# A stack of three preactivated convolutions and one rational filter: two batches instead of one take a tile from products shared by pixel pairs

## The chip, the cores and the metric

The kernel runs on one core of a Trainium2 chip. The metric is the device time of one execution in microseconds. The engines have rows of their own: TensorE (PE, with its weight loads as PEld), VectorE (DVE), ScalarE (ACT), GpSimd (POOL) and SyncE (SP), which only issues DMAs. Each engine works its row in the order in which the program lists it; an instruction that waits holds up everything behind it on that engine. DMAs are issued from SP, ACT and POOL and stand in those rows too.

## The reference

Four layers follow one another, each `x = x + layer(norm(x))` on `x` of 4 batches x 32 x 32 pixels x 16 channels. `norm` is a group norm over 8 groups of 2 channels. The first three layers have this form, with `M` and `Wp` of 1024 x 1024 and a 3x3 kernel `G` of its own for each of the 1024 output pixels:

```
first   = einsum('ijpq,bpqc->bijc', M2, inputs)
K       = transpose(G, (2, 3, 4, 0, 1, 5)).reshape(kh, kw, c, h*w*f)
shifted = conv(inputs, K, 'SAME').reshape(b, h, w, h, w, f)
diff    = relu(inputs[:, :, :, None, None, :] - shifted)
second  = einsum('ijpq,bpqijc->bijc', W2, diff)
return first - second
```

So each output pixel has its own convolution over the whole image, a Relu, and a weighted sum over the 1024 pixels. That makes 1024 x 16 filter outputs over 1024 pixels for each batch and layer. The last layer is a two-dimensional filter given as a ratio of polynomials, worked out as an impulse response and applied by matmuls.

## The kernel before

**Blocks and tiles.** The 1024 x 16 filters of a layer are 128 blocks of 128. A *tile* is one block for one batch: 128 filters on the partitions, 1024 pixels as two halves of 512 columns in PSUM. `iteration` (line 653) makes one tile: TensorE computes it, then VectorE *evicts* it with one instruction (line 658), which takes the minimum with 0, multiplies by the weights `wts` and sums over the pixels into `acc`.

**Two kinds of tile.** `SHARED` (line 19) says for each batch which kind it is. A `direct` tile (line 594) runs the nine taps over all 512 columns of a half: two float32 products of four taps each, `f`, and one of the ninth tap as high and low pieces in float32r, `g` (line 609). A `shared` tile (line 614) works on pairs of neighbouring pixels: products common to both are computed once on 256 columns into a PSUM buffer `both` (line 625), ScalarE copies that to SBUF as `both_sb` (line 629), TensorE computes the pixels' own part (line 637), and VectorE adds `both_sb` to it in PSUM (line 645) before the eviction. Only batch 3 is shared. All PSUM tiles, `pt`, come from one pool of four buffers (line 51); a shared tile takes two of them.

**Order.** `passes` (line 85) lists what runs. A layer has its first 12 blocks for batches 0 and 1, then the same blocks for batches 2 and 3, then the 104 middle blocks with all four batches in turn, then the last 12 blocks for 0 and 1 and again for 2 and 3. The split gives time to make the next layer's image of two batches while the other two still run. `order` is the list of all 1536 tiles, `now["at"]` the place in it, `begin[u]` where chunk `u` of four blocks begins, and `need` where a chunk's other taps are needed.

**Work beside the tiles.** It is written as generators. After every tile `iteration` calls `step` (line 586), which moves each one on; `until(at)` waits for a place in the order. So the code says after which tile an instruction is listed, and each engine keeps that order:

- `four_taps` (485) loads `f` of a chunk and has GpSimd subtract the middle tap.
- `other_taps` (499) loads the tap table `raw`; after 4 to 7 tiles GpSimd subtracts the middle tap and adds (lines 506 to 508), one tile later ScalarE casts `hi` (512), one later GpSimd makes `lo` (514) and issues eight DMAs to DRAM (519). `piece_loads` (524) loads them back as `g` on SP, one tile of 128 x 512 for a chunk without a shared batch, six with one (12 DMAs).
- `w_loads` (576) loads the weights, 1 MB for two blocks, from six buffers.
- `make_image` (309), `store_image` (342) and `load_image` (380) make the next layer's image of a pair of batches: norm, copies and differences on ScalarE, GpSimd and VectorE, three DMAs to DRAM, and 28 DMAs back, taken in turn by SP and POOL for batches 0 and 1 and by SP, POOL and ACT for 2 and 3.
- `first_term` (419) makes the product with `M`; `impulse_response` (724), beside layer 0's middle, makes the filter of the last layer, much of it on GpSimd.

**The opening.** The host gives the taps of batches 0 and 1 unnormalised. `first_images` (192) normalises and masks them in SBUF for the first pass; its `rest` makes the image of batches 2 and 3 during that pass. The loads are listed from line 864 on.

Of the kernel before, what the change touches and what calls it, by code (L numbers as in the profile page):

```python
# [18 lines left out]
SHARED = (False, False, False, True)  # L19
# [17 lines left out]
def conv_stack_kernel(ctx, tc, x, M, W, first_w, first_f, first_g, F, E, h0, coef, cst, dft, idp, idq, out):  # L37
# [10 lines left out]
    ge = ctx.enter_context(tc.tile_pool(name="ge", bufs=1))  # L48
    junkp = ctx.enter_context(tc.tile_pool(name="junk", bufs=1))
# [22 lines left out]
    ye = [const.tile([P, row[a]], F32, name=f"ye{a}") for a in range(2)]  # L72
    for t in (*yp, *ye):
        nc.gpsimd.memset(t, 0.0)
# [10 lines left out]
    passes = [  # L85
        (blks, batches)
        for layer in range(3)
        for blks, batches in (
            (range(layer * NBLK, layer * NBLK + END), (0, 1)),
            (range(layer * NBLK, layer * NBLK + END), (2, 3)),  # L90
            (range(layer * NBLK + END, (layer + 1) * NBLK - END), (0, 1, 2, 3)),
            (range((layer + 1) * NBLK - END, (layer + 1) * NBLK), (0, 1)),
            (range((layer + 1) * NBLK - END, (layer + 1) * NBLK), (2, 3)),
        )
    ]
# [9 lines left out]
    now = {"at": 0}  # L105
# [86 lines left out]
    def first_images(nine, g9):  # L192
# [21 lines left out]
        def last_tap(b):  # L214
            v, v8 = nine[:, b], ims_of(b)[1].rearrange("p l m -> p (l m)")
            m = neg[:, B + b : B + b + 1]
            nc.vector.tensor_scalar(v8, v, m, rstd[:, B + b : B + b + 1], ALU.add, ALU.mult)
            nc.vector.tensor_scalar(v, v, m, rlo[:, b : b + 1], ALU.add, ALU.mult)
            nc.vector.scalar_tensor_tensor(v8, v8.bitcast(F32), sign, v, ALU.mult, ALU.add)
            nc.gpsimd.memset(  # L220
                ims_of(b)[1].rearrange("p l (cc x) -> p (l cc) x", x=S)[:, :, S - 1 :].bitcast(F32), 0.0
            )

        def first_taps(u):
            part = g9[:, bass.ts(u, GC * P)]
            nc.scalar.copy(gn0[u], part)
            for r in (32, 96):
                lo = gn0[u][r : r + 32]
                nc.vector.tensor_tensor(lo, part[r : r + 32], lo.bitcast(F32), ALU.subtract)
            gt[u] = [gn0[u]]  # L230
# [30 lines left out]
        minus_mid(fours[0][:, 1].rearrange("r (n f) -> r n f", f=C), mid, nc.vector)  # L261
# [4 lines left out]
        for _ in range(2):  # L266
            next(norm)
        dft(0, 1)
# [8 lines left out]
        normalise(0, 0, nc.vector)  # L277
        clear(0, 0)
        normalise(0, 1, nc.scalar)
        clear(0, 1)  # L280
# [3 lines left out]
        last_tap(0)  # L284
        for k in range(2):
            normalise(1, k, nc.vector)
            clear(1, k)
        last_tap(1)

        def rest():  # L290

            yield
            yield
            first_taps(1)
            yield
            pair = lambda a: (xs[:, 2 * a : 2 * a + 2], *(t[:, 2 * a : 2 * a + 2] for t in (neg, rstd)))
            yield from store_image(1, *pair(1))
            yield
            load_image(0, 1)
            copy_out(1)  # L300
            yield
            center(0, *pair(0))
            yield
            copy_out(0)
            nc.vector.tensor_copy(avg_r, avg)
# [3 lines left out]
    def make_image(layer, a, xt):  # L309

        xt = xt[:, 2 * a : 2 * a + 2]
        neg, rstd = yield from group_norm(xt)
        yield from store_image(a, xt, neg, rstd)
        yield
        load_image(layer + 1, a)
        copy_out(a)
# [25 lines left out]
    def store_image(a, xt, neg, rstd):  # L342
# [27 lines left out]
        for b, v in enumerate(kinds):  # L370
            to = kinds_of(ye[a], a, b)
            nc.gpsimd.tensor_copy(to[96:, :, 1:], v[96:, :, :3])
            nc.scalar.copy(to[:32, :, :3], v[:32, :, 1:])
        rows = img[a]
# [5 lines left out]
    def load_image(layer, a):  # L380

        moves = []
        of = lambda t: t.rearrange("p l k m -> p l (k m)")
        for b in range(2):
# [26 lines left out]
        queues = (nc.sync, nc.gpsimd, nc.scalar)[: 2 + a]  # L411
        for n, (to, src) in enumerate(moves):
            queues[n % len(queues)].dma_start(out=to, in_=src)  # L413
# [71 lines left out]
    def four_taps(u):  # L485

        at = max(begin[u] - 30, begin[u - 2] if u > 2 else 0)
        if u == 1:
            at = 2
        yield from until(at)  # L490
        load_f(u)
        yield from until(min(max(at + 8, begin[u] - 16), begin[u] - 2))
        minus_mid(fours[u][:, 1].rearrange("r (n f) -> r n f", f=C), mid)
# [5 lines left out]
    def other_taps(q, at):  # L499

        layer, ch = divmod(q, NBLK // GC)
        yield from until(at[0])
        raw = ge.tile([96, 3, 2 * P], F32, tag="raw", name="raw")
        nc.sync.dma_start(out=raw.rearrange("r k n -> r (k n)"), in_=E[layer][ch])
        yield from until(at[1])
        minus_mid(raw[:, 1].rearrange("r (n f) -> r n f", f=C), mid_e)
        for k in (1, 2):
            nc.gpsimd.tensor_tensor(raw[:, 0], raw[:, 0], raw[:, k], ALU.add)  # L508
        yield from until(at[1] + 1)
        both = raw[:, 0::2]  # L510
        hi, lo = (ge.tile([96, 2, 2 * P], F32R, tag=tag, name=tag) for tag in ("hi", "lo"))
        nc.scalar.copy(hi, both)  # L512
        yield from until(at[1] + 2)
        nc.gpsimd.tensor_tensor(lo, both, hi.bitcast(F32), ALU.subtract)  # L514
        to = gd[q % len(gd)]
        for k, t in enumerate((hi, lo)):
            for u in range(2):
                for slot in range(2):
                    nc.gpsimd.dma_start(  # L519
                        out=to[slot, :, k, :, bass.ts(u, 2 * P)],  # L520
                        in_=t[48 * u : 48 * u + 48, slot].bitcast(F32),
                    )

    def piece_loads(u):

        q, first, sharing = uses[u]
        yield from until(max(begin[u - 1], first - 12))
        tiles = [gn.tile([P, GC * P], F32R, tag=f"g{n}", name=f"g{n}") for n in range(6 if sharing else 1)]
        gt[u] = tiles
        to = gd[q % len(gd)]  # L530
        rows = (1, 0, 2), (1, 2, 0), (1, 1, 1), (0, 0, 0), (0, 1, 1), (0, 2, 2)
        for t, (slot, *dys) in zip(tiles, rows):
# [6 lines left out]

    tasks = []  # L540
    at = 0, 1
    for q in sorted(need, key=need.get):
        tasks.append((at[0], other_taps(q, at)))
        following = [k for k in sorted(need, key=need.get) if need[k] > need[q]][:1]
        for k in following:
            first = max(need[k] - 26, at[1] + 3)
            at = first, max(first + 4, min(first + 7, need[k] - 9))
# [28 lines left out]
    def w_loads():  # L576
        while len(wts) < len(w_first):
            k = len(wts)
            yield from until(w_first[k] - (24 if k > 5 else 10))
            while not w_free():  # L580
                yield
            list(load_w())
# [69 lines left out]

    def iteration(layer, acc):
        blk, b, u = order[now["at"]]
        assert blk // NBLK == layer
        pt = (shared if SHARED[b] else direct)(layer, u, blk, b)
        junk = junkp.tile([P, S * S], F32, tag="junk", name="junk")
# [9 lines left out]
        now["at"] += 1  # L667
        step()

    def conv_layer(layer, xt, finish, side=(), also=iter(())):  # L670
# [11 lines left out]
        for job, (blks, batches) in enumerate(passes[5 * layer : 5 * layer + 5]):  # L682
            for blk in blks:
                for _ in batches:
                    iteration(layer, acc)
                if job == 2:
# [5 lines left out]
            if job > 2:  # L692
                a = batches[0] // 2
# [170 lines left out]
    with tc.tile_pool(name="st", bufs=1) as st:  # L864
        table = st.tile([P, B], F32, name="table")
# [3 lines left out]
        image_tiles(0, 0)  # L869
        image_tiles(0, 1)  # L870
        nine = st.tile([P, 2, 4 * PX], F32, name="nine")
        g9 = st.tile([P, 2 * GC * P], F32, name="g9")
        first_part = 4 * P + 2 * NCH
        coefs = st.tile([P, coef.shape[1]], F32, name="coefs")
        for part in (slice(0, first_part), slice(first_part, coef.shape[1])):
            nc.sync.dma_start(out=coefs[:, part], in_=coef[:, part])
# [4 lines left out]
        nc.scalar.dma_start(out=g9[:, : GC * P], in_=first_g[:, : GC * P])  # L881

        def load_first(b):
            size = 8 * PX
            for to, at in ((ims[0, b][0].rearrange("p l k m -> p (l k m)"), 0), (nine[:, b], 8 * PX)):
                nc.sync.dma_start(out=to, in_=first_f[:, b, at : at + size])
                size = 4 * PX

        load_f(0)
        load_first(0)  # L890
        list(load_w(2))
        load_first(1)
        nc.sync.dma_start(out=g9[:, GC * P :], in_=first_g[:, GC * P :])
# [15 lines left out]
    FIRST = 24  # L909
# [18 lines left out]
    def of_pair(a, k, q):  # L928
# [3 lines left out]
            (("pair", a), 2 * i + half, y(31 - TQ * k - q - i + 16 * half - FIRST), k, q + i)  # L932
# [28 lines left out]
    def norm3(_, a, xt):  # L961
# [15 lines left out]
        if a == 0:  # L977
            yq = work.tile([P, 16 * (31 + S - FIRST)], F32, name="yq")
# [20 lines left out]
        for y in (  # L999
            late["yp"][:, a, :, 31 - FIRST :],  # L1000
# [21 lines left out]
    tp = ctx.enter_context(tc.tile_pool(name="tp", bufs=TB))  # L1022

# [5 lines left out]
    def toeplitz():  # L1029
        for k in held[:TB]:  # L1030
# [29 lines left out]
    for n, slot in enumerate(then):  # L1060
        if n in (2, 4, 5):
            k = {2: 4, 4: 3, 5: last}[n]
            list(load_toeplitz(k, toeplitz_tile(k, tp)))
# [173 lines left out]
```

## Time and profile before

| | us |
|---|---|
| three runs, median (lowest to highest) | 3047.37 (3042.73 to 3047.81) |
| the profiled execution, its own time | 3047.96 |
| its span, first to last instruction | 3046.2 |
| L609 matmuls of direct tiles, float32: busy, mean of one | 2239.4, 0.592 |
| L637 matmuls of shared tiles, float32 and float32r: busy | 509.8 and 503.4 |
| L658 evictions: busy, mean of one, count | 1880.8, 1.224, 1536 |
| L645 additions of `both_sb`: busy, mean, count | 473.1, 1.232, 384 |
| L629 copies to `both_sb`: busy, mean, count | 224.9, 0.586, 384 |
| L512 casts on ScalarE: busy, mean, count | 59.3, 0.618, 96 |
| GpSimd: busy in all | 1070.6 |

A line of a group in the profile has the code line, the engine, the operation, `out<-in` and the shapes. A timeline row has the start and length in us, the engine, the code line, the operation, how many instructions of that kind are merged in it, and in brackets how long the engine had stood idle before and what ended that. Busy times of TensorE overlap, as its two halves of 64 rows work at once; the distance between the first matmuls of two tiles is the time of a tile. The granted clock of TensorE is 1.00 in the middle of the layers and 0.91 in the first 100 us.

### The profile page before, as it was taken

Reading aid. Unit: us, or ns where it says so; the run is one execution under the profiler, and the core shown is the slowest. Engines: PE = TensorE matmul, PEld = TensorE weight load, DVE = VectorE, ACT = ScalarE, POOL = GpSimd, SP = SyncE. Lnnn points to the kernel's source line nnn. Section 1 sums busy time; section 2 is a strip of 40 time slices with the busy share of each in tenths; the row PEclk is TensorE's granted clock in tenths of the full one; section 3 lists DMA queues with packets and bytes.
Section 4 is the critical chain, followed back from the end, with each engine's and each line's share of the span. In section 5 each row is a group of like instructions: output and inputs, shape, how many; then the busy total and the mean of one; then the engine's idle time right before and its main releaser. Section 6 shows DMA issues by size and latency. Waiting matters only on the chain.

```text
span 3046.2 us, 53601 instructions
## 1 busy us (share of the span) xinstructions
PE 2982.4 (98%) x20884; PEld 2192.1 (72%) x20884; DVE 2412.9 (79%) x3639; ACT 307.5 (10%) x555; POOL 1070.6 (35%) x1517
## 2 busy tenths in 40 slices
PE   7999999999999899999999999989999999999998
PEld 4765666788887576678888888757567888888874
DVE  5878888888887787788888888769788888888873
ACT  1110110000001011000000100101000000000000
POOL 5435663232332433432323233343333233332300
PEclk8999999999999999999999999999999999999998
DMA  8887676656675898766666676589777776857634
GB/s 233 230 207 185 158 189 167 178 154 169 162 164 146 209 224 200 182 155 168 165 158 173 150 180 150 157 198 235 197 179 178 167 185 163 199 151 180 151 107 80
DMA packets 235589, 531.82 MB, mean 175 GB/s; under 512 B 83672, under 2 KB 93496, under 8 KB 209992
## 3 DMA queue, kind: packets, MB, share of 16 engines
q1 hardware_dynamic: 162832, 472.72, 61.3%
q0 software_dynamic: 66480, 47.05, 6.7%
q10 hardware_dynamic: 6024, 8.63, 1.4%
q8 instruction: 165, 2.70, 0.4%
q14 instruction: 88, 0.72, 0.1%
HBM read 481.67 MB, written 45.92 MB: 173 GB/s over the span
## 4 chain that ended last, share of the span: by engine, by line
PE 84%; DVE 3%; DMA 2%; issue 1%; SPq 0%; ACT 0%; POOL 0%; DVEq 0%; POOLq 0%; ACTq 0%
PE pt L609 65%; PE pt L637 14%; PE pt L625 3%; DVE junk L658 2%; PE pt L952 1%; DVE pt L645 1%; DMA f<-img 1%; DMA t<-hd 1%; PE pt L445 0%; DMA g<-gd 0%; SPq L535 0%; DMA raw<-in_E_dram 0%; SPq L413 0%; DVE st L150 0%; POOL raw L508 0%
## 5 line engine op out<-in xcount | busy, mean ns | idle before, releaser
L609 PE MATMUL pt<-f,f 64*128 64x512 f32 x9216 | 2239.4, 592 | 10.3 <-DVE junk L658 4.0
L658 DVE SCALAR_TENSOR_TENSOR junk<-pt,w 128x1024 f32<-128x1024 f32 x1536 | 1880.8, 1224 | 372.7 <-PE pt L609 256.1
L609 PEld LDWEIGHTS pt<-f,f 64*128 64x128 f32 x9216 | 1149.1, 187 | 503.6 <-issue 264.6
L609 PE MATMUL pt<-n,g 64*128 64x480 f32 x2304 | 997.0, 779 | 6.3 <-DMA g<-gd 6.2
L645 DVE TENSOR_TENSOR pt<-pt,both_sb 128x1024 f32<-128x1024 f32 x384 | 473.1, 1232 | 195.2 <-PE pt L637 164.4
L637 PE MATMUL pt<-f,f 64*128 64x256 f32 x3072 | 509.8, 378 | 3.5 <-DVE junk L658 1.2
L637 PE MATMUL pt<-n,g 64*128 64x256 f32 x3072 | 503.4, 372 | 0.0
L629 ACT COPY both_sb<-pt 128x512 f32<-128x512 f32 x384 | 224.9, 586 | 2350.5 <-PE pt L625 2265.3
L609 PEld LDWEIGHTS pt<-n,g 64*128 64x128 f32 x2304 | 314.9, 188 | 188.5 <-issue 102.9
L475 POOL TENSOR_TENSOR raw<-raw,cs 96x256 f32<-96x256 f32 x96 | 69.8, 727 | 908.6 <-DMA raw<-in_E_dram 908.3
L637 PEld LDWEIGHTS pt<-n,g 64*128 64x128 f32 x3072 | 370.2, 188 | 6.3
L514 POOL TENSOR_TENSOR lo<-raw,hi 96x512 fp32r<-96x512 f32 x96 | 121.9, 1270 | 529.3 <-ACT hi L512 529.3
L637 PEld LDWEIGHTS pt<-f,f 64*128 64x128 f32 x3072 | 293.6, 186 | 4.8 <-PE pt L625 2.6
L625 PEld LDWEIGHTS pt<-n,g 64*128 64x128 f32 x2304 | 230.8, 186 | 83.1 <-issue 35.9
L625 PE MATMUL pt<-n,g 64*128 64x256 f32 x2304 | 230.3, 279 | 20.2 <-ACT both_sb L629 20.2
L519 POOL DMA_DIRECT2D gd<-lo x384 | 226.8, 597 | 12.8 <-DMA f<-img 8.1
L519 POOL DMA_DIRECT2D gd<-hi x384 | 229.6, 603 | 3.2 <-issue 3.2
L475 POOL TENSOR_TENSOR f<-f,cs 128x512 f32<-128x512 f32 x113 | 145.6, 1289 | 192.3 <-DMA f<-in_F_dram 167.5
L508 POOL TENSOR_TENSOR raw<-raw 96x256 f32<-96x256 f32 x192 | 139.5, 727 | 15.1
L658 DVE DVE_READ_ACCUMULATOR junk<-pt,w 128x1 f32 x1536 | 127.8, 83 | 0.0
L512 ACT CAST hi<-raw 96x512 fp32r<-96x512 f32 x96 | 59.3, 618 | 189.2 <-POOL raw L508 189.0
L461 POOL DMA_DIRECT2D fd<-ft x48 | 25.2, 533 | 44.2 <-ACT ft L453 27.2
(131 smaller groups left out, 341.2 us busy)
## 6 DMA issues: line engine op xcount, KB each, us to landing
w<-in_W_dram SPq DMA_DIRECT2D x188, 1024.0 KB, 12.1
g<-gd SPq DMA_DIRECT2D x1184, 128.0 KB, 4.3
f<-in_F_dram SPq DMA_DIRECT2D x114, 512.0 KB, 3.6
raw<-in_E_dram SPq DMA_DIRECT2D x96, 288.0 KB, 9.3
gd<-hi POOLq DMA_DIRECT2D x384, 48.0 KB, 4.2
gd<-lo POOLq DMA_DIRECT2D x384, 48.0 KB, 4.5
mt<-in_M_dram SPq DMA_DIRECT2D x12, 512.0 KB, 12.7
w<-in_M_dram SPq DMA_DIRECT2D x12, 512.0 KB, 8.0
```

The lines of the kernel that those rows point to most:

```text
L475: engine.tensor_tensor(v, v, m.unsqueeze(1).to_broadcast([v.shape[0], v.shape[1], C]), ALU.subtract)
L508: nc.gpsimd.tensor_tensor(raw[:, 0], raw[:, 0], raw[:, k], ALU.add)
L512: nc.scalar.copy(hi, both)
L514: nc.gpsimd.tensor_tensor(lo, both, hi.bitcast(F32), ALU.subtract)
L519: nc.gpsimd.dma_start(out=to[slot, :, k, :, bass.ts(u, 2 * P)], in_=t[48 * u : 48 * u + 48, slot].bitcast(F32),)
L609: nc.tensor.matmul(pt[:, half, px], lhsT=w[rows, at], rhs=rhs, start=k == 0, stop=k == 2)
L625: nc.tensor.matmul(both[:, half], lhsT=w[rows, at], rhs=ni[rows, dy : dy + 4, 2], start=dy == 0, stop=dy == 2)
L629: nc.scalar.copy(sb, both)
L637: nc.tensor.matmul(pt[:, half].rearrange("p (r k m) -> p k r m", k=2, m=16)[:, k], lhsT=w[rows, at], rhs=rhs, start=k == j == 0, stop=k == ...
L645: nc.vector.tensor_tensor(v, v, sb.rearrange("p h (r m) -> p (h r) m", m=16).unsqueeze(2).to_broadcast([P, 32, 2, 16]), ALU.add,)
L658: nc.vector.scalar_tensor_tensor(junk, pt.rearrange("p h m -> p (h m)"), 0.0, wts[blk // 2][:, blk % 2, :], ALU.min, ALU.mult, accum_out=a ...
L952: nc.tensor.matmul(rows.rearrange("n (j r) -> n j r", j=C)[:, :, 8 * cc :], lhsT=y(cc).rearrange("p q b -> p (q b)"), rhs=ts[k][q][:, :, : ...
```

## The change

1. Batch 1 becomes shared too; a block then has two direct tiles (0, 2) and two shared ones (1, 3). In the last and first 12 blocks the pass of batches 0 and 1 has one of each, as that of 2 and 3 had, and needs all six `g` tiles.
2. `by_pool` picks one eviction in four: in the middle batch 2, in layer 0's first 12 blocks batch 1, in the other end passes the direct batch of every second block. `by_gpsimd` does it in three steps: ScalarE writes Relu(-pt) to SBUF as `r`, GpSimd multiplies by the weights in place, and ScalarE, listed four tiles later by `finish_sums`, copies `r` with scale -1 and sums it into `acc`.
3. In `other_taps` the cast `hi` moves from ScalarE to GpSimd and everything from the subtraction to the eight DMA issues is listed at one place. `raw` has two buffers and is asked for up to 34 tiles ahead of need, and worked on 15 ahead. `lo` takes its place.
4. `piece_loads` asks for the five tiles of shared batches as soon as their own buffers allow, and for the first one as before.
5. The first pass of layer 0 has batches 0 and 2 (`FIRST`), both direct, and the second 1 and 3, both shared. `rest` makes an image of both pairs, one after the other, and loads only batch 1 and batch 3 of them. The loads of the opening come in another order, some tiles move to other buffers, and the first `f` loses its middle tap on GpSimd instead of VectorE.
6. `load_image` issues one batch's 14 DMAs after each of two tiles, on SP and POOL alone. While an image is stored and loaded (`now["image"]`), `w_loads` issues nothing.

The core of the diff:

```diff
-SHARED = (False, False, False, True)
+SHARED = (False, True, False, True)
+FIRST = (0, 2)
...
+    er = ctx.enter_context(tc.tile_pool(name="er", bufs=2))
+    rp = ctx.enter_context(tc.tile_pool(name="rp", bufs=2))
...
-        normalise(0, 0, nc.vector)
+        normalise(FIRST[0], 0, nc.vector)
...
+            for a in range(2):
+                pair = slice(2 * a, 2 * a + 2)
+                at = xs[:, pair], neg[:, pair], rstd[:, pair]
+                later = [b for b in range(2) if 2 * a + b not in FIRST]
+                if later:
+                    yield from store_image(a, *at)
+                    yield
+                    yield from load_image(0, a, later)
...
-        queues = (nc.sync, nc.gpsimd, nc.scalar)[: 2 + a]
-        for n, (to, src) in enumerate(moves):
-            queues[n % len(queues)].dma_start(out=to, in_=src)
+            queues = nc.sync, nc.gpsimd
+            for n, (to, src) in enumerate(moves):
+                queues[n % len(queues)].dma_start(out=to, in_=src)
+            yield
+        now["image"] -= 1
...
-        raw = ge.tile([96, 3, 2 * P], F32, tag="raw", name="raw")
+        raw = er.tile([96, 3, 2 * P], F32, tag="raw", name="raw")
...
-        yield from until(at[1] + 1)
         both = raw[:, 0::2]
-        hi, lo = (ge.tile([96, 2, 2 * P], F32R, tag=tag, name=tag) for tag in ("hi", "lo"))
-        nc.scalar.copy(hi, both)
-        yield from until(at[1] + 2)
+        hi, lo = ge.tile([96, 2, 2 * P], F32R, tag="hi", name="hi"), both.bitcast(F32R)
+        nc.gpsimd.tensor_copy(hi, both)
         nc.gpsimd.tensor_tensor(lo, both, hi.bitcast(F32), ALU.subtract)
...
+        first = max(need[q] - 34, done[-2])
+        at = first, max(first + 3, need[q] - 15, done[-1])
...
-            while not w_free():
+            while not w_free() or now["image"]:
...
+    def by_pool(blk, b):
+        if END <= blk % NBLK < NBLK - END:
+            return b == 2
+        if blk < END:
+            return b == 1
+        return not SHARED[b] and blk % 2 == 0
+
+    def by_gpsimd(pt, blk, to):
+        r = rp.tile([P, S * S], F32, tag="r", name="r")
+        nc.scalar.activation(r, pt.rearrange("p h m -> p (h m)"), AF.Relu, scale=-1.0)
+        nc.gpsimd.tensor_tensor(r, r, wts[blk // 2][:, blk % 2, :], ALU.mult)
+        sums_due.append((now["at"] + 4, r, to))
+
+    def finish_sums(all=False):
+        while sums_due and (all or sums_due[0][0] <= now["at"]):
+            _, r, to = sums_due.pop(0)
+            nc.scalar.activation(r, r, AF.Copy, scale=-1.0, accum_out=to)
...
         pt = (shared if SHARED[b] else direct)(layer, u, blk, b)
+        if by_pool(blk, b):
+            by_gpsimd(pt, blk, acc[b // 2][:, b % 2, blk % NBLK : blk % NBLK + 1])
+            return
...
                     iteration(layer, acc)
+                    now["at"] += 1
+                    finish_sums()
+                    step()
```

## The prediction

> **What bounds the kernel now.** I read the page's engine shares and its chain first, then a stretch of windows, then one block in the timeline, then the costliest groups, the waits, and the stretches at a layer's end.
>
> ```profile
> PE 2982.4 (98%) x20884; PEld 2192.1 (72%) x20884; DVE 2412.9 (79%) x3639; ACT 307.5 (10%) x555; POOL 1070.6 (35%) x1517
> PE pt L609 65%; PE pt L637 14%; PE pt L625 3%; DVE junk L658 2%; PE pt L952 1%; DVE pt L645 1%; DMA f<-img 1%; DMA t<-hd 1%; PE pt L445 0%; DMA g<-gd 0%; SPq L535 0%; DMA raw<-in_E_dram 0%; SPq L413 0%; DVE st L150 0%; POOL raw L508 0%
> ...
> 2500.00:2900.00 400.00, 400.00 (x2762) 326.08 (x2758) 328.01 (x481) 37.32 (x65) 128.13 (x177) 1.00 0.68 170
> ```
>
> The chain is matmuls: 65% direct tiles (line 609), 17% shared ones (637, 625). In the window (PE, weight loads, DVE, ACT, POOL, then clock and DMA) TensorE is busy all 400 us at clock 1.00, VectorE 82%, GpSimd 32%. So in the middle of a layer TensorE sets the pace and a tile's price is the distance between tile starts:
>
> ```profile
> 1502.55 0.52 PE L625 MATMUL pt<-n,g 64*128 64x256 f32 x5
> ...
> 1504.24 0.59 PE L609 MATMUL pt<-f,f 64*128 64x512 f32 x1
> ...
> 1506.17 1.88 PE L609 MATMUL pt<-f,f 64*128 64x512 f32 x7
> ...
> 1510.04 0.52 PE L625 MATMUL pt<-n,g 64*128 64x256 f32 x5
> ```
>
> A shared tile takes 1504.24 - 1502.55 = 1.69 us, a direct one (1510.04 - 1504.24) / 3 = 1.933; three and one make a block of 7.49. Where only batches 2 and 3 run, VectorE is the pace:
>
> ```profile
> 2952.23 1.23 DVE L645 TENSOR_TENSOR pt<-pt,both_sb 128x1024 f32<-128x1024 f32 x1
> 2953.49 1.23 DVE L658 SCALAR_TENSOR_TENSOR junk<-pt,w 128x1024 f32<-128x1024 f32 x1
> ...
> 2954.83 1.23 DVE L658 SCALAR_TENSOR_TENSOR junk<-pt,w 128x1024 f32<-128x1024 f32 x1
> ...
> 2955.98 1.23 DVE L645 TENSOR_TENSOR pt<-pt,both_sb 128x1024 f32<-128x1024 f32 x1
> ```
>
> An addition holds it 1.26, an eviction 1.34 before another eviction and 1.15 before an addition: 3.75 per pair of tiles, where TensorE needs 3.62. Last, the ScalarE wait at a layer's end and the GpSimd work of one chunk:
>
> ```profile
> 1015.44 0.62 ACT L512 CAST hi<-raw 96x512 fp32r<-96x512 f32 x1 [15.27 <-POOL raw L508]
> 1015.96 0.57 ACT L629 COPY both_sb<-pt 128x512 f32<-128x512 f32 x1
> ...
> 1500.88 0.72 POOL L475 TENSOR_TENSOR raw<-raw,cs 96x256 f32<-96x256 f32 x1 [11.69 <-DMA raw<-in_E_dram]
> 1501.69 1.53 POOL L508 TENSOR_TENSOR raw<-raw 96x256 f32<-96x256 f32 x2
> 1511.90 1.27 POOL L514 TENSOR_TENSOR lo<-raw,hi 96x512 fp32r<-96x512 f32 x1 [8.68 <-ACT hi L512]
> 1513.12 2.38 POOL L519 DMA_DIRECT2D gd<-hi  x4
> 1515.49 2.36 POOL L519 DMA_DIRECT2D gd<-lo  x4
> 1517.87 1.30 POOL L475 TENSOR_TENSOR f<-f,cs 128x512 f32<-128x512 f32 x1
> ```
>
> The cast stood in ScalarE's row before a `both_sb` copy and waited for a late tap load; TensorE stood still twice for it, 20.2 us together.
>
> **What the change takes away.** Batch 1 becomes shared: in the middle stages 3 layers x 104 blocks x (1.933 - 1.69 = 0.243) = -75.9 us. Five end passes of batches 0 and 1 (three at a layer's end, two at its start), 12 blocks each: -14.6. Five passes of batches 2 and 3 fall from VectorE's 3.75 to TensorE's 3.62, since half of the direct tiles leave VectorE: 5 x 12 x 0.13 = -7.8. The cast leaves ScalarE's row: -20.2. Together -118.5.
>
> **Whether the other engines hold that pace.** VectorE per middle block: evict, add, evict, add, evict = 1.15 + 1.26 + 1.15 + 1.26 + 1.34 = 6.16 of TensorE's 7.25. ScalarE: two copies of 0.59, the new Relu (the 128x1024 PSUM copy of line 788 took 1.02), the summing copy. The last has no row: at least the 1.02, at most that plus two of VectorE's 0.08 accumulator reads and a small ACTIVATE of 0.20, so 1.02 to 1.4; I take 1.2, near the plain copy. Sum 3.4. Relu stands nowhere in this trace; a table load for it and another back (1.28 each, line 867) would make 6.0, still under 7.25. GpSimd: the product is 128x1024; 256 columns take 0.73, 512 take 1.29, so 1.29 + 2 x 0.56 = 2.41 (2.3 to 2.6, by the rows' spread). `hi` on GpSimd: its 32x480 copy took 0.58, the two-operand form 1.27; one operand, so 0.62, bounds 0.6 and 1.27. A chunk of four blocks then holds 9.7 of products, a burst of 2.3 + 0.62 + 1.2 + 4.75 plus gaps = 9.1 (two adds, cast, subtraction, eight DMA issues, now in one piece) and 1.3 for `f`: 20 of 29.0 us. On average all fit; what counts is the order in the queues.
>
> The Trainium skill (GPSIMD Engine Reference, 4.1) speaks against the product's place: elementwise work belongs on VectorE, GpSimd being about twice as slow with two inputs. The row agrees, 2.41 against 1.22; on VectorE it would close the block at 7.5, no faster than now. The skill (SBUF — State Buffer, two separate sides) also says that GpSimd and a VectorE instruction with two SBUF inputs lock each other out. The evictions read one input from PSUM, and that of 1501.08 took 1.23 beside GpSimd's 1501.69 as others do alone; with a lock 384 products would cost VectorE up to 384 x (2.41 - 1.09 idle) = 500 us, by the row nothing.
>
> **What it adds on the path.** The summing copy waits in ScalarE's row for the product; behind it stand the next Relu and the next `both_sb` copy, for which VectorE's addition waits, and TensorE for its PSUM buffer.
>
> *Chunk by chunk.* From the chunk's first tile: Relu 5.9 to 6.9, product to 9.4, burst to 18.5, second product to 20.9, its sum to 22.1; the third block's Relu, due at 20.4, ends at 23.1, its copy at 23.7, so an addition due at 22.15 comes 1.55 late. VectorE regains 1.09 per block. If PSUM's four buffers go round in fixed order, TensorE loses 1.1 us per chunk (the tile that starts at 25.4 wants a buffer evicted at 26.3, the rest a block on); if they are handed out as they come free, nearly nothing. The trace has both: the tile at 2951.12 waited for the buffer taken four before, that at 1016.59 for a copy of the one taken three before. I take 0.8 for each of 78 middle chunks, +62 (0 to 86); a dear `hi` adds 0.65 each, 50 more.
>
> *Layer ends.* In the pass of batches 2 and 3 before layers 1 and 2 GpSimd has three bursts (27.3), three `f` (3.9), six products (14.5), the image's arithmetic (3.0) and 7 issues per batch of 0.56 (7.8): 56.5 in a pass of 43.5. The 13 over goes to TensorE as above, with 2 for GpSimd waits on DMA (one of 3.36 at 1003.45): +15, and +4 in the next pass, whose image issues also stand before a product; two boundaries, +38 (10 to 55).
>
> *Opening.* First pass: the waits of 2.4 (`f`, 37.05) and 6.2 (`g`, 61.52) go; but three bursts and now two images stand in GpSimd's row, 44 us from 24 on, so the third `f` comes some 6 late and batch 3's image 7 late: near -2 together. Second pass, batches 1 and 3: the Relu of a shared tile waits for VectorE's addition, and the next `both_sb` copy stands behind it. Addition 1.26, Relu 1.02, copy 0.59, addition 1.26, eviction 1.15 close a ring of 5.3 us per block; 12 blocks are 64 against today's 46.2 (78.81 to 125.06): +17. Without the ring VectorE's 3.67 would hold: -2. Sum +15 (-4 to +25).
>
> *Layer 0's filter.* Its GpSimd work comes in lumps, four of 5.7 (eight products of 0.72 a block) and four of 4.3 (copies of 1.08), where a block leaves GpSimd 2.25 idle; with its DMA issues and VectorE's reciprocals waiting on it, +24 (5 to 35).
>
> **At no cost**: five `g` tiles more in 15 chunks, 10 issues x 0.62 on SP, making 9.4 of 14.5 us there, hidden as in today's passes of batches 2 and 3 (if not, like the 6.2 us wait for `g`); tap loads earlier and double buffered (GpSimd's 908 us wait was idle time); `w` loads held for some five tiles while an image loads, asked for 10 to 24 tiles ahead (else 12.1 to landing); images without ScalarE's queue, inside the 7.8 above.
>
> **Sum**: 3046.2 - 118.5 + 62 + 38 + 15 + 24 = 3066.7 us of span. The profiled execution took 3047.96, 1.8 more than its span; the runs' median is 3047.37, so 3068 to be set against it.
>
> **Rivals.** *The hold-ups drown* (faster): buffers come as they are free, so 0.25 per chunk (20), boundaries 26, filter 18, opening 15: 3046 - 118.5 + 79 = 3006.5. For it speaks the wait at 1016.59 and GpSimd's 31% idle; against it VectorE's 1.09 us of slack. It decides if a chunk costs under 0.5. *The burst weighs more* (slower): `hi` at 1.27 and fixed buffers, 1.75 per chunk, 137, boundaries 45, filter 30, opening 15: 3155. For it speaks that no one-operand row has this strided input. *GpSimd and VectorE block each other*, so the products do not relieve VectorE: 7.5 or more per block, 3046 - 20 + 77 of the other terms = 3100 upward; the row at 1501.08 speaks against it.
>
> **How the numbers follow.** Forecast 0.42 (own range 3042 to 3100), drowned 0.39, heavier burst 0.14, blocking 0.05. A change under 0.2% (6 us) can't be told from none here; 0.06 of the forecast and 0.04 of the first rival fall there. Slower 0.36 + 0.14 + 0.05 = 0.55, same 0.10, faster 0.35. The range reaches from below the first rival's 3006.5, with a free filter and boundaries, to near the second: 2985 to 3130.
>
> **What would show it.** Middle blocks with tile starts 7.25 apart, and once per chunk a wait of `pt` on an eviction or copy, with a summing copy behind GpSimd before it: right. Blocks at 7.25 throughout: the first rival. VectorE evictions longer than 1.23: blocking. The second pass near 5.3 per block confirms the ring. The forecast is wrong if PSUM never holds TensorE in the middle, or if the casts on GpSimd take over 1 us.

## The result, and the profile after

The changed kernel took 3121.96 us (median of four runs, 3117.49 to 3125.03) against 3045.18 for the kernel before: ratio 1.025 (1.0238 to 1.0262), slower by 77 us. The forecast was 3068, slower by 21. The profiled execution took 3124.87 us, its span 3123.1. The page after, its engine shares and five groups (line, engine, operation, tiles, count, then busy time, mean ns, and the idle time before them with what ended it):

```profile
PE 2945.3 (94%) x25492; PEld 2175.0 (70%) x25492; DVE 2407.1 (77%) x3253; ACT 1243.3 (40%) x2002; POOL 2047.4 (66%) x2026
...
L683 POOL TENSOR_TENSOR r<-r,w 128x1024 f32<-128x1024 f32 x384 | 909.5, 2369 | 919.1 <-ACT r L682 907.0
L699 DVE SCALAR_TENSOR_TENSOR junk<-pt,w 128x1024 f32<-128x1024 f32 x1152 | 1410.5, 1224 | 95.9 <-PE pt L627 26.4
L663 DVE TENSOR_TENSOR pt<-pt,both_sb 128x1024 f32<-128x1024 f32 x768 | 945.4, 1231 | 545.4 <-ACT both_sb L647 279.1
...
L682 ACT ACTIVATE r<-pt 128x1024 f32<-128x1024 f32 x384 | 391.9, 1021 | 514.3 <-PE pt L627 474.4
L689 ACT ACTIVATE r<-r 128x1024 f32<-128x1024 f32 x384 | 407.1, 1060 | 392.8 <-POOL r L683 392.7
```

TensorE is busy for 37 us less than before (2982.4) and is now idle for 6% of the span. VectorE's instructions are no longer than before (1.224 and 1.231 us), so it does not suffer from GpSimd's products beside it. The new instructions have the lengths that the forecast gave them: product 2.37 (2.41), Relu 1.02 (1.02), summing copy 1.06 with a separate read of its accumulator of 0.19 beside what follows (1.2). What stands out is the last column: ScalarE waits 392.7 us for products.

The time by stretch, from the tile starts of both traces. The forecast's terms are put on the stretches where their parts lie; a "boundary" is the last pass of a layer (batches 2, 3) and the two first passes of the next:

| stretch | before | after | change | forecast |
|---|---|---|---|---|
| opening, up to the first middle | 123.1 | 150.1 | +27.0 | +15 |
| middle of layer 0 | 794.0 | 809.5 | +15.5 | -25.3 + 20.7 + 24 = +19.4 |
| middles of layers 1 and 2 | 1572.9 | 1572.8 | -0.1 | -9.3 |
| three passes of 0, 1 that end a layer | 139.2 | 137.9 | -1.3 | -8.8 |
| two boundaries | 304.2 | 340.2 | +36.0 | -20.2 + 38 - 12.1 = +5.7 |
| last pass and tail | 112.8 | 112.5 | -0.3 | -1.6 |

The sum is +76.9 against +20.5. Over half of the 56 us between them lie in the boundaries. In the middle, one chunk of the changed kernel, on four engines:

```profile
1499.61 1.77 POOL L528 DMA_DIRECT2D gd<-hi  x3
...
1501.37 2.36 POOL L528 DMA_DIRECT2D gd<-raw  x4
...
1503.74 2.38 POOL L683 TENSOR_TENSOR r<-r,w 128x1024 f32<-128x1024 f32 x1
...
1506.15 1.06 ACT L689 ACTIVATE r<-r 128x1024 f32<-128x1024 f32 x1 [3.19 <-POOL r L683]
1507.21 1.00 ACT L682 ACTIVATE r<-pt 128x1024 f32<-128x1024 f32 x1
...
1508.12 0.58 ACT L647 COPY both_sb<-pt 128x512 f32<-128x512 f32 x1
...
1508.72 1.23 DVE L663 TENSOR_TENSOR pt<-pt,both_sb 128x1024 f32<-128x1024 f32 x1 [2.33 <-ACT both_sb L647]
...
1511.37 1.95 PE L627 MATMUL pt<-f,f 64*128 64x512 f32 x7 [0.45 <-DVE junk L699]
```

The chain is the one forecast: the end of the burst holds the product until 1503.74, the summing copy waits 3.19 us for it, Relu and `both_sb` copy stand behind, VectorE's addition comes 2.33 us late, and three tiles on TensorE has no free PSUM buffer. The pair of tiles that ends with the 0.45 us wait took 4.26 us in place of 3.62, the next two 3.75 and 3.70.

At the first boundary of the changed kernel GpSimd is late, then everything behind it:

```profile
1040.51 1.03 ACT L682 ACTIVATE r<-pt 128x1024 f32<-128x1024 f32 x1 [1.69 <-PE pt L627]
...
1047.01 2.36 POOL L528 DMA_DIRECT2D gd<-raw  x4
...
1052.56 1.04 POOL L423 DMA_DIRECT2D n<-img  x2
1052.87 1.25 SPq L591 DMA_DIRECT2D w<-in_W_dram  x2
1053.61 2.35 POOL L683 TENSOR_TENSOR r<-r,w 128x1024 f32<-128x1024 f32 x1
1054.21 0.54 SPq L495 DMA_DIRECT2D f<-in_F_dram  x1
1054.86 17.03 SPq L545 DMA_DIRECT2D g<-gd  x12
...
1056.00 1.06 ACT L689 ACTIVATE r<-r 128x1024 f32<-128x1024 f32 x1 [11.00 <-POOL r L683]
...
1058.11 1.01 PE L643 MATMUL pt<-n,g 64*128 64x256 f32 x6 [6.47 <-ACT r L682]
...
1075.85 0.46 PE L627 MATMUL pt<-n,g 64*128 64x480 f32 x1 [4.55 <-DMA g<-gd]
```

Burst and image issues stand before one product for 12 us, and TensorE waits 6.47. Then, in the first pass of the next layer, it waits 4.55 for a `g` tile, whose loads stand in SP's queue behind two `w` of 1 MB; the twelve issues take 17.03 us where a middle's take some 8. The DMA engines from the last pass of layer 0 to the middle of layer 1, after and before:

```profile
DMA packets 19232, 36.02 MB, mean 209 GB/s; under 512 B 6032, under 2 KB 8400, under 8 KB 18128
```
```profile
DMA packets 16573, 32.16 MB, mean 212 GB/s; under 512 B 4889, under 2 KB 7737, under 8 KB 15411
```

The same rate, 3.86 MB more, 18 us at 210 GB/s; the two boundaries grew by 20.6 and 15.4 us. So the questions were: is the burst the cause in the middle, what holds the boundaries, and what the opening.

### The profile page after: what moved, and what is told of

Read it like the earlier page. It is cut to its first block, busy times and chain, and to the rows that moved or that the text cites. A ratio compares the mean times of both kernels' runs of the same rounds, so it can differ in the third digit from the quotient of the medians.

```text
span 3123.1 us, 65218 instructions
## 1 busy us (share of the span) xinstructions
PE 2945.3 (94%) x25492; PEld 2175.0 (70%) x25492; DVE 2407.1 (77%) x3253; ACT 1243.3 (40%) x2002; POOL 2047.4 (66%) x2026
## 5 line engine op out<-in xcount | busy, mean ns | idle before, releaser
L627 PE MATMUL pt<-f,f 64*128 64x512 f32 x6144 | 1489.8, 598 | 69.5 <-DVE junk L699 68.0
L683 POOL TENSOR_TENSOR r<-r,w 128x1024 f32<-128x1024 f32 x384 | 909.5, 2369 | 919.1 <-ACT r L682 907.0
L699 DVE SCALAR_TENSOR_TENSOR junk<-pt,w 128x1024 f32<-128x1024 f32 x1152 | 1410.5, 1224 | 95.9 <-PE pt L627 26.4
L663 DVE TENSOR_TENSOR pt<-pt,both_sb 128x1024 f32<-128x1024 f32 x768 | 945.4, 1231 | 545.4 <-ACT both_sb L647 279.1
L655 PE MATMUL pt<-f,f 64*128 64x256 f32 x6144 | 968.0, 380 | 27.5 <-ACT both_sb L647 13.2
L655 PE MATMUL pt<-n,g 64*128 64x256 f32 x6144 | 947.6, 372 | 8.9 <-DMA g<-gd 8.9
L655 PEld LDWEIGHTS pt<-n,g 64*128 64x128 f32 x6144 | 659.2, 188 | 35.3 <-DMA g<-gd 9.6
L627 PE MATMUL pt<-n,g 64*128 64x480 f32 x1536 | 625.4, 778 | 15.5 <-DMA g<-gd 14.1
L682 ACT ACTIVATE r<-pt 128x1024 f32<-128x1024 f32 x384 | 391.9, 1021 | 514.3 <-PE pt L627 474.4
L689 ACT ACTIVATE r<-r 128x1024 f32<-128x1024 f32 x384 | 407.1, 1060 | 392.8 <-POOL r L683 392.7
L643 PEld LDWEIGHTS pt<-n,g 64*128 64x128 f32 x4608 | 415.7, 187 | 196.7 <-issue 147.4
L643 PE MATMUL pt<-n,g 64*128 64x256 f32 x4608 | 422.5, 279 | 26.4 <-ACT r L682 24.4
L627 PEld LDWEIGHTS pt<-n,g 64*128 64x128 f32 x1536 | 170.0, 188 | 184.8 <-issue 170.5
```

What stands on the lines that cost most here:

```text
L627: nc.tensor.matmul(pt[:, half, px], lhsT=w[rows, at], rhs=rhs, start=k == 0, stop=k == 2)
L643: nc.tensor.matmul(both[:, half], lhsT=w[rows, at], rhs=ni[rows, dy : dy + 4, 2], start=dy == 0, stop=dy == 2)
L655: nc.tensor.matmul(pt[:, half].rearrange("p (r k m) -> p k r m", k=2, m=16)[:, k], lhsT=w[rows, at], rhs=rhs, start=k == j == 0, stop=k == ...
L663: nc.vector.tensor_tensor(v, v, sb.rearrange("p h (r m) -> p (h r) m", m=16).unsqueeze(2).to_broadcast([P, 32, 2, 16]), ALU.add,)
L682: nc.scalar.activation(r, pt.rearrange("p h m -> p (h m)"), AF.Relu, scale=-1.0)
L683: nc.gpsimd.tensor_tensor(r, r, wts[blk // 2][:, blk % 2, :], ALU.mult)
```

## The experiments

Medians stand beside runs of the kernel before on the same chip; "ratio" is to these.

**Middle, 1: the burst in two pieces.**

```diff
         nc.gpsimd.tensor_tensor(lo, both, hi.bitcast(F32), ALU.subtract)
+        yield from until(at[1] + 4)
         to = gd[q % len(gd)]
...
-        at = first, max(first + 3, need[q] - 15, done[-1])
-        done.append(at[1] + 1)
+        at = first, max(first + 3, need[q] - 19, done[-1])
+        done.append(at[1] + 5)
```

> The eight DMA issues of a tap burst on GpSimd stand four tiles behind its arithmetic, so that a product can go between them; the burst begins four tiles earlier. Theory A (the middle's loss is the one long burst in front of a product, which the summing copy in ScalarE's row passes on to the next Relu and copy): a product is held by 4.8 us at most in place of 9.1, the summing copy's wait of 3.2 us per chunk nearly goes, and most of the some 1.0 to 1.26 us that a chunk loses against 4 x 7.25 comes back: 40 to 80 us less than the changed kernel, about 3040 to 3080. Theory B (the loss in the middle is not from the burst but from the tighter ring of evictions, copies and PSUM buffers): within 10 us of 3122.

Measured: 3027.99, ratio 0.9935 (0.9919 to 0.9952), 94 us less than the change and faster than the kernel before. One block of its middle:

```profile
1501.83 2.42 POOL L529 DMA_DIRECT2D gd<-hi  x4
...
1504.23 2.36 POOL L529 DMA_DIRECT2D gd<-raw  x4
...
1506.61 2.38 POOL L684 TENSOR_TENSOR r<-r,w 128x1024 f32<-128x1024 f32 x1
...
1509.44 1.06 ACT L690 ACTIVATE r<-r 128x1024 f32<-128x1024 f32 x1
...
1512.29 1.02 ACT L683 ACTIVATE r<-pt 128x1024 f32<-128x1024 f32 x1 [1.70 <-PE pt L628]
```

The summing copy has no wait, Relu waits for TensorE again. The middles of layers 1 and 2 take 761.6 us (after: 787.2 and 785.7). Theory A holds, and the gain is above its 40 to 80 us: the three middles give 74, the passes of 0 and 1 behind them 7, and the opening and the boundaries fall too.

**Middle, 2: the summing copy later.**

```diff
-        sums_due.append((now["at"] + 4, r, to))
+        sums_due.append((now["at"] + (6 if END <= blk % NBLK < NBLK - END else 4), r, to))
```

> The summing copy of a middle product is put six tiles behind its tile in ScalarE's row, not four; nothing else moves. Theory A: the product behind a burst ends some 18 us after its tile starts, the copy is reached at about 13 in place of 9, its wait falls by about 3.6 us per chunk to near nothing on average, so 40 to 80 us less in all, 3040 to 3080. Theory B: within 10 us of 3122. Should the next Relu, which now needs the buffer that this copy frees one tile before, become late instead, slower by up to 20.

Measured: 3035.1, ratio 0.9957 (0.994 to 0.9973), 87 us less than the change, again above theory A's range. Middles of 761.8 us with the burst in one piece; ScalarE's waits for products fall to

```profile
ACT r L689 <- POOL r L683: 80.9, 34, 10.5
```

(total, times, longest; after it was 392.7 in 178). The long burst as such costs next to nothing there: what cost was a copy that stood too early in an in-order queue behind it.

**Opening: the Relu behind the next copy.** `by_gpsimd` of a batch 1 tile is called after the matmuls and the copy of the next tile:

```diff
         pt = (shared if SHARED[b] else direct)(layer, u, blk, b)
+        while relus_due:
+            by_gpsimd(*relus_due.pop())
+        if blk < END and b == 1:
+            relus_due.append((pt, blk, acc[b // 2][:, b % 2, blk % NBLK : blk % NBLK + 1]))
+            return
```

> In the second pass of layer 0 alone, the Relu of a batch 1 tile is put behind the next tile's both_sb copy in ScalarE's row. Theory E (this pass runs at 5.21 us a block because addition, Relu, copy, addition and eviction follow one another in a ring): the ring is cut, VectorE's 3.67 us per block holds, so 12 x 1.5 = 18 us less at most, and 8 to 18 with the pass's GpSimd burst and its wait for g left: 3104 to 3114. Rival (the pass is bound by GpSimd's product, burst and loads): within 5 us of 3122.

Measured: 3108.73, ratio 1.0203 (1.0188 to 1.0218), 13 us less. The changed kernel's ring, as forecast, in two blocks 5.21 apart, and the same place with the Relu moved, 3.54 apart:

```profile
112.06 1.02 ACT L682 ACTIVATE r<-pt 128x1024 f32<-128x1024 f32 x1 [2.19 <-DVE pt L663]
...
117.27 1.02 ACT L682 ACTIVATE r<-pt 128x1024 f32<-128x1024 f32 x1 [2.19 <-DVE pt L663]
```
```profile
112.99 1.03 ACT L682 ACTIVATE r<-pt 128x1024 f32<-128x1024 f32 x1 [0.52 <-DVE pt L663]
...
116.53 1.02 ACT L682 ACTIVATE r<-pt 128x1024 f32<-128x1024 f32 x1 [0.52 <-DVE pt L663]
```

The second pass falls from 75.8 to 63.6 us. It stays far above the 44.2 of before: TensorE waits 8.4 us for `g` at its start, as it did after (8.6).

**Boundary, 1: `w` not held.**

```diff
-            while not w_free() or now["image"]:
+            while not w_free():
```

> The loads of w are no longer held back while an image is loaded. Theory C (at a layer's start two loads of w, 1 MB each, held back and then issued together, stand in SP's queue just ahead of the g tiles that the shared batch 1 now needs there; TensorE's waits of 4.6 and 3.0 us on g and the low clock after them come from this): 8 to 10 us less at each of the two boundaries, and part of the 8.6 us wait for g in the opening's second pass: 15 to 28 us less, 3094 to 3107. Theory D (g is late because its burst on GpSimd and the image issues are late, the w loads are only near by): within 6 us of 3122, or a few us slower as the images land later.

Measured: 3126.89, ratio 1.0258 (1.0243 to 1.0274). TensorE's waits for `g` fall from 23.0 to 10.1 us in all and the first passes get shorter (56.5 and 55.5 for 61.7 and 58.1), but the last passes longer by 2.2 and 3.7, and the first boundary stays at 172.1. The hold did not make the loss; it only says in which pass it shows.

**Boundary, 2 to 4: fewer loads, no products, neither.** One edit gives the shared tile of batch 1 the direct tile's `g` in the first pass of layers 1 and 2, the other gives every eviction to VectorE:

```diff
-        if sharing:
+        blk, b, _ = order[first]
+        lean = blk >= END > blk % NBLK and b < 2
+        if sharing and not lean:
...
+        if lean:
+            gt[u][1:] = 5 * [gt[u][0]]
```
```diff
-        if by_pool(blk, b):
+        if False:
```

> In the first pass of layers 1 and 2 (batches 0 and 1, 12 blocks) the shared tile of batch 1 reads the one g tile that the direct tile reads, for all six: the five more g tiles of each chunk are not loaded there, so part of the taps is replaced by others, and every instruction on the engines stays. Theory F (a layer's start is bound by the bytes that the DMA engines carry: from the last pass of a layer to the middle of the next they moved 36.0 MB in 172 us against 32.2 MB in 152 us before, about 210 GB/s both times): 3.84 MB less at each boundary, 15 to 20 us less each, 3082 to 3092. Theory G (the products, Relus and summing copies in GpSimd's and ScalarE's rows hold the start of a layer): the pass stays at 58 to 62 us, within 8 us of 3122.

> Every eviction is VectorE's again; the shared tiles of batch 1, the casts on GpSimd and the opening stay. Both theories: the middle goes to VectorE's 1.15 + 1.26 + 1.34 + 1.15 + 1.26 + 1.34 = 7.50 a block, so 780 to 787 us per middle, as the changed kernel has now (786) and the kernel before had; the first middle 12 to 20 us less since its filter shares GpSimd with no product; the second pass 12 x 4.82 in place of 12 x 5.21, 5 less. Theory F: the layer starts stay within 5 us of theirs, 3085 to 3105. Theory G: they fall to near 152 us each, 3050 to 3070.

> Both of the last two edits together: every eviction on VectorE, and the first pass of layers 1 and 2 reads one g tile for all six, so its five more g tiles a chunk are not loaded and part of the taps is replaced by others. From the last pass of a layer to the middle of the next the changed kernel takes 172.1 and 168.1 us, without products 163.1 and 162.3, with fewer loads 163.5 and 162.2, and the kernel before 151.4 and 153. If products and loads are two causes that add up (theories F and G both, each a half): 152 to 157 each, 3072 to 3080 in all. If they are one queue seen twice (whatever comes last sets the start): 158 to 163, 3085 to 3092.

Measured: 3112.61 (ratio 1.0211, 1.0196 to 1.0226), 3092.1 (1.0146, 1.0131 to 1.0161) and 3076.72 (1.0105, 1.009 to 1.012). The boundaries:

| | first, us | second, us | MB in the first | GB/s |
|---|---|---|---|---|
| before | 151.5 | 152.7 | 32.16 | 212 |
| after | 172.1 | 168.1 | 36.02 | 209 |
| fewer loads (e5) | 163.5 | 162.2 | 32.38 | 198 |
| no products (e6) | 163.1 | 162.3 | 35.40 | 217 |
| neither (e9) | 152.5 | 153.4 | 31.78 | 208 |

The two causes add up: each alone is worth 6 to 9 us per boundary and 9 to 11 once the other is gone, and together they are nearly what the boundary had lost. Neither theory alone held. Fewer loads are fewer bytes and also fewer issues in SP's row; these runs don't tell the two apart. And e9 has the cast on GpSimd, and is no faster there than the kernel before: the forecast's 20.2 us are missing.

**Boundary, 5 and 6: the cast alone.** The kernel before with the cast on GpSimd, and then with half of `w` not loaded at the layer's start (the evictions of these blocks read the half that is):

```diff
-        nc.scalar.copy(hi, both)
+        nc.gpsimd.tensor_copy(hi, both)
...
-        n = 2 * S * S // parts
+        n = 2 * S * S // (2 if layer and at < 6 else parts)
```

> The kernel before, with nothing changed but the tap cast, which stands in GpSimd's row. The forecast's term: TensorE's two waits of 9.9 and 10.3 us behind the cast in ScalarE's row go, 20 us less than before, about 3025. Rival (the boundary is bound by bytes, or the cast's wait moves to GpSimd's row and f or g come later): 0 to 10 us less, 3036 to 3046.

> The kernel before with the cast on GpSimd; for the first 12 blocks of layers 1 and 2 only the first half of each w tile is loaded and both its blocks are weighed with it, so that half of these weights is left out and 3 MB less is moved at each of two boundaries. With the cast alone the boundaries (last pass of a layer to the middle of the next) stayed at 156.0 and 154.1 us against 155.4 and 156.7, though TensorE's 20.2 us behind the cast had gone: 9.4 and 7.3 us of waits for g came in their place. Theory F (bytes): 3 MB at some 215 GB/s are 14 us, so 10 to 14 less at each boundary, about 3014 to 3022. Theory J (the chain image loads, tap load, burst on GpSimd, g, one after the other): within 6 us of 3042.

Measured: 3041.84, ratio 0.9985 (0.9976 to 0.9995): some 4 us, not 20. Before, TensorE had these two waits:

```profile
1016.59 1.01 PE L625 MATMUL pt<-n,g 64*128 64x256 f32 x6 [9.90 <-ACT both_sb L629]
...
2001.31 1.01 PE L625 MATMUL pt<-n,g 64*128 64x256 f32 x6 [10.26 <-ACT both_sb L629]
```

They go: the last pass of layer 0 is shorter by some 12. But the first pass of layer 1 is longer by as much:

```profile
1009.00 0.57 SPq L573 DMA_DIRECT2D w<-in_W_dram  x1
...
1010.42 2.04 SPq L535 DMA_DIRECT2D g<-gd  x2
...
1012.55 1.20 SPq L573 DMA_DIRECT2D w<-in_W_dram  x2
...
1013.85 0.54 SPq L483 DMA_DIRECT2D f<-in_F_dram  x1
...
1014.60 4.77 SPq L535 DMA_DIRECT2D g<-gd  x2
...
1021.92 0.74 PE L609 MATMUL pt<-n,g 64*128 64x480 f32 x1 [9.43 <-issue]
```

TensorE comes earlier and stands 9.43 us before a matmul that reads `g`. With 3 MB of `w` less: 3029.63, ratio 0.9939 (0.9924 to 0.9953), 12 us less, and that wait is

```profile
1014.64 0.45 PE L609 MATMUL pt<-n,g 64*128 64x480 f32 x1 [0.98 <-issue]
```

with every instruction in its old order. The boundaries of the two runs are 152.1 and 150.2, then 141.7 and 144.2 us (29.07 MB in the first; the expectations count from shared tile to shared tile, 3.9 us more). The first boundary gains 10 us and the second 6, where theory F asked for 10 to 14 at each and theory J for nearly none: bytes are the larger part, not all of it.

**Boundary, 7 and 8: `w` by ScalarE's queue**, for the first 24 blocks of layers 1 and 2, on the version of e8 below and on e7.

```diff
-            nc.sync.dma_start(out=wt.rearrange("p k m -> p (k m)")[:, part], in_=src)
+            queue = nc.scalar if layer and at < 12 else nc.sync
+            queue.dma_start(out=wt.rearrange("p k m -> p (k m)")[:, part], in_=src)
```

> The version with the burst in two pieces, later sums and the second pass's Relu behind the copy; the loads of w for the first 24 blocks of layers 1 and 2 go by ScalarE's queue in place of SP's. Theory H (the g tiles of a layer's first chunk wait in SP's queue behind two to three w of 1 MB): TensorE's waits of about 4 to 5 us for g at each layer's start and the low clock after them go, 8 to 12 us less at each of two boundaries, 2985 to 2995. Theory F (the DMA engines' bytes alone set it, whichever queue they stand in): within 6 us of 3009. If ScalarE's row is held by the w that wait for their buffers, slower by 5 to 15.

> The kernel before with the cast on GpSimd and, in addition, the loads of w for the first 24 blocks of layers 1 and 2 by ScalarE's queue. With the cast alone TensorE's 20.2 us behind it went, and 9.4 and 7.3 us of new waits came at the layers' starts, for g. Theory H: those g stood behind w; the new waits go and the 20 us come through, 3015 to 3027. Theory F: within 6 us of 3042.

Measured: 3056.6 (ratio 1.0034, 1.0022 to 1.0046) and 3066.12 (1.0066, 1.0049 to 1.0083), 48 and 24 us more than without the move, worse than any of the expectations. In e11 ScalarE's row:

```profile
987.87 0.58 ACT L630 COPY both_sb<-pt 128x512 f32<-128x512 f32 x1 [1.25 <-PE pt L626]
1002.07 0.54 ACTq L574 DMA_DIRECT2D w<-in_W_dram  x1
1002.71 1.07 ACT L630 COPY both_sb<-pt 128x512 f32<-128x512 f32 x2 [14.25 <-DMA g<-gd]
```

The `w` issue holds two copies until 1002.07, 14 us after the copy before it. So the runs can't tell the order in SP's queue from the bytes; they show what a load costs whose issue waits in a compute engine's row. The Trainium skill (DMA: Bandwidth & Descriptors, Issuing engines are not separate DMA queues) says that DMAs run on the same 16 DMA engines whichever engine starts them, and that another issuer saves only the time of the issue; neither run shows a gain that would speak against it.

**Together.** The burst in two, the later sums and the later Relu; then, on top of that, products only in the middles, the opening and the passes of 0 and 1 that end a layer; then e8 with half of `w` left out as in e13. The edit of e12, beside those shown:

```diff
-        return not SHARED[b] and blk % 2 == 0
+        return b == 0 and blk % NBLK > END and blk % 2 == 0
```

> The burst in two pieces, the middle's summing copies two tiles later and the second pass's Relu behind the next copy, together. Theory A: the first two take away the same wait (middles of 761.6 us in either run), so together they give little more than one of them, 756 to 761.6 per middle; the Relu gives its 13 us: 3000 to 3018. If each took away a different wait, the middles would go near 754 and the total to 2990.

> The version with the burst in two pieces, later sums and the second pass's Relu behind the copy; at the layers' ends and starts products stay only in the pass of batches 0 and 1 that ends a layer, the other passes' evictions are VectorE's. Theory G: the stall of 5 to 6 us behind burst, image issues and product in the last pass of layers 0 and 1 goes with its low clock, and half of it shows: 6 to 12 us less at each of two boundaries, 2985 to 2997. Rival (g is late next, so TensorE waits for it one pass later): within 6 us of 3009.

> The version with the burst in two pieces, later sums and the second pass's Relu behind the copy, with the same half of w left out for the first 12 blocks of layers 1 and 2. Theory F: 10 to 14 us less at each of two boundaries (165.5 and 167.0 now), 2980 to 2990. Theory J: within 6 us of 3009.

Measured: 3008.79 (ratio 0.9881, 0.9865 to 0.9898), 3007.8 (0.9878, 0.9863 to 0.9893) and 2999.77 (0.9844, 0.9828 to 0.9861). e8 leaves nothing out and beats both kernels, 113 us under the change. Its middles take 761.6 us, so e1 and e2 take away the same wait. In e12 the stall in a layer's last pass goes (52.0 us for 62.6) and the first pass of the next gets longer by 7.0, as the rival of theory G had it: the boundary stays at 166 us. In e14, e8 with less of `w`, the boundaries fall by 5 to 6 us, less than theory F asks; what bounds the rest there is open.

## Why the prediction was wrong

The direction came true, though with a sum of 20 us made of terms of over 100 either way, and nearly every error lay on one side of it. Several steps held. **Middle, tile prices**: without the hold-up a middle is 786.5 - 761.6 = 24.9 us shorter, 74.7 for three against 75.9. **VectorE, ScalarE and GpSimd row by row**: every duration was within its bounds; `hi` took 0.607 us (0.62), so the rival of a dear burst had no ground, though its total lay near; and the rival of engines blocking each other fell with the unchanged 1.224 us: the lock that the Trainium skill (SBUF — State Buffer, SBUF: two separate sides) describes is for VectorE instructions with two SBUF inputs or in a 2-port mode, and these rows, with one input in PSUM, show no lock. **The hold-up chunk by chunk** was the mechanism, by the queue that the forecast named: (786.4 - 761.6) / 26 = 0.95 us, not 0.8, so 74 for 62; the rival in which hold-ups drown (under 0.5) is refuted. The passes of 0 and 1 that end a layer have it too, in their first block: 46.0 us after, 43.5 with the burst split, so 7.5 of the 8.8 us of gain there went. This was not in the sum. **The filter** came to 15.6 (first middle less the others, 23.1 against 7.5), not 24.

**The step that failed is the boundary**, twice. "The cast leaves ScalarE's row: -20.2": the wait left, as e7 shows, and 4 us came in all, 2 of them in the boundaries. What was next to be late was the next layer's `g`, behind `w`; e13 shows it by taking bytes away. The forecast read the 9.9 and 10.3 us as the price of a row, where they were slack that a second, later limit would have taken. "At no cost: five `g` tiles more": they were costed as issues on SP, 9.4 of 14.5 us, and not as bytes. A first pass has three chunks, so 30 more DMAs of 128 KB, 3.6 to 3.9 MB by the table; windows of the kernel before show that this pass of layer 1 already moved 202 GB/s at a DMA share of 0.81 (the pass behind it 231 at 0.91). e5, and e9 against e6, show 6 to 11 us for that at each boundary. That it is the bytes and not the issues is argued from that share and from e13, where bytes alone went; no run took away the issues of `g` alone. The forecast's +38 for GpSimd's work at the layer ends was near for the last passes (63.8 and 62.1 measured, 63.9 and 64.8 by its terms) and right in kind (in e6 they fall to 50.8 and 51.2). The loss shows in the first passes behind them: 61.7 and 58.1 us, where its terms give 47.0 - 2.9 + 4 = 48.1.

**Opening**: the ring was read well, 5.21 us a block against 5.3. Its pass took 75.8 and not 64, since TensorE waited 8.6 us for `g` in batch 1's first tile, whose last two loads were issued at 80.53 us behind seven image loads in SP's queue, and two summing copies waited 3 us each for products behind bursts; this is read from the rows, no run took it away. The forecast also set the pass against a wrong 46.2 us: 125.06 is the start of the middle's second tile, the middle begins at 123.06, and the pass of before took 44.2. The first pass gained 4.5 in place of 2.

The total of the errors, 56 us: boundaries 30, opening 12, middles of layers 1 and 2 9, the passes that end a layer 8, the rest -3.

## What to carry to other kernels

A wait that a change removes is worth only what lies between it and the next thing that is late: before it is counted, look in the same stretch for the next load or row, and divide the bytes that must pass there by the rate that the stretch already has. Added loads are costed in bytes against the DMA share of their own stretch, not only in issues. This gives an upper bound: 2.7 to 3.6 MB at 210 GB/s are 13 to 17 us, and taking them away gained 5 to 11 at a boundary (e5, e9, e13, e14). And where one engine's result comes back into another's in-order queue, its place there (six tiles behind in place of four: 87 us) can matter more than the work itself.

## What was not expected of the hardware

A long stall of TensorE costs more than its length. Windows of the changed kernel around the 6.47 us wait (after PE, weight loads, DVE, ACT and POOL come the granted clock, the DMA share and GB/s):

```profile
1050.00:1054.00 4.00, 1.64 (x9) 0.83 (x6) 0.00 (x0) 0.00 (x0) 3.98 (x8) 1.00 0.71 175
1054.00:1058.00 4.00, 0.00 (x0) 0.00 (x0) 0.00 (x0) 2.00 (x4) 3.18 (x2) 0.75 0.98 210
1058.00:1061.40 3.40, 3.29 (x22) 2.95 (x24) 2.70 (x4) 1.99 (x4) 3.19 (x3) 0.50 1.02 222
1061.40:1064.00 2.60, 2.60 (x14) 1.25 (x12) 2.56 (x4) 0.28 (x2) 2.38 (x4) 0.72 1.05 227
```

The clock falls to 0.50 during the wait, and stays there for the first 3.4 us of matmuls and a part of the next 2.6. The Trainium skill (TensorE: Matmul & The Clock Gate, Part 1) says that the clock is halved after an idle window of about 3.4 us and comes back after as long a busy one; these rows agree. The 0.45 us waits of the middle leave the granted clock at 1.00, and yet the two pairs of tiles after one of them took 0.13 and 0.08 us more than 3.62:

```profile
1511.14 0.08 DVE L699 DVE_READ_ACCUMULATOR junk<-pt,w 128x1 f32 x1
...
1514.89 0.08 DVE L699 DVE_READ_ACCUMULATOR junk<-pt,w 128x1 f32 x1
...
1515.12 1.95 PE L627 MATMUL pt<-f,f 64*128 64x512 f32 x7
```

VectorE's evictions end at 1511.22 and 1514.97, 3.75 apart, and TensorE starts a direct tile 0.15 us after each (1511.37 and 1515.12). So TensorE seems to follow VectorE's late chain for one pair more, in waits too short to stand in brackets; this is read from the rows and not tested.
